# Graph attention with conditional features: the setup of a one-core kernel re-planned

## The chip, the cores and the metric

The kernel runs on one core of a Trainium2 chip. The metric is the device time of one execution in microseconds (us); the time of a kernel is the median of its runs. The engines of the core that matter here are TensorE (PE in the profile, with its weight loads as PEld), VectorE (DVE), ScalarE (ACT), GpSimd (POOL) and SyncE (SP), which in this kernel issues nearly all DMAs. Each engine takes its instructions in the order in which the program lists them for it.

## The reference

There are 16 batches of 512 nodes with 512 features, 16 heads of width 32, and two relations d. Only the first 20 nodes of a batch act as keys and values. Cut to what matters:

```python
row_zero = v.sum(-1) == 0                       # a node whose features sum to zero
q_exp = where(row_zero[..., None], 0.0, q[:, None, :])
self_feat = concat([v, q_exp], -1) @ W_self.T + b_self
output = self_feat
for d in range(2):
    A = (adj if d == 0 else swapaxes(adj, 1, 2))[:, :, :20, :]
    mask, bias = A.sum(-1) > 0, A @ w_bias + b_bias
    kv = self_feat[:, :20]
    qh = self_feat @ Wq[d].T + bq[d]            # split over heads
    kh = kv @ Wk[d].T + bk[d]                   # split over heads
    w = softmax(where(mask, qh . kh / sqrt(32), NEG) + bias)
    output += per_head(w @ kv) @ Wout[d] + bout[d]
return v + relu(output)
```

The condition vector q enters each node's features by one term, W_self's second half times q, which is dropped for nodes whose row sum is zero. The kernel holds that decision as a *row flag* per node (0 or 1). All arithmetic is in float32.

## The kernel before

**What is done once.** The query projection is folded into the keys: for every batch, the 20 keys of both relations and all 16 heads are multiplied by Wq once, so that the scores of a node are one product of its self features with a table g of 512 x 640 per batch. The setup (lines 347 to 630) makes these tables for all 16 batches, the value rows, a bias term per key, and half of the self features of batch 0. The main loop (from line 658) then runs over 16 batches b and four tiles nt of 128 nodes: it makes the self features of the tiles to come (`self_feat`), the scores of this tile, softmax, and in tile 2 the attention output of the batch before.

**The order is by hand.** The program stands in `tc.manual_schedule()`: every engine executes in the order of the text. A tile buffer is one of `bufs` slots of its tag, handed out in turn; an instruction that writes to a slot waits until all that used the slot's former tile is done, DMAs included.

**The setup's stages.**

- *Front.* SP loads the key nodes' features `xkv` and the weights `ws_v` in four pieces of 128 rows, with the condition `q_sb`, its weights `ws_q` (1 MB) between pieces 1 and 2 (lines 394 to 414), and then everything else: key weights, query weights, x of batch 0, adjacency, output weights, x of batch 1 (`load_x(1)`, line 415). Eight matmuls on constants keep TensorE busy meanwhile (line 384). The key nodes' features accumulate in `kv_ps`; between pieces 1 and 2 stands the product of q with `ws_q` (line 435).
- *Key rows.* `key_rows(d, jc)` (line 470): four matmuls of 128x320 into a bank of `ps_acc`, which ScalarE moves to `khT`. There are eight.
- *Bursts.* `keys(runs)` (line 543): the 64 halves of the table are taken three at a time, so there are 22 bursts, 0 to 21, the last with one half. A burst fills two PSUM pairs (`ps_s`, both of its buffers). ScalarE then empties pair 0 and VectorE pair 1 into a stage tile `st` (lines 563 to 569), and the next burst can begin only when both are empty. When a stage is full, SP writes its share of batch 0 to `g0` in SBUF, of batch 1 to `g1_d` and of the other 14 batches to `g_d`, both in DRAM (lines 572 to 576). `st` has four slots.
- *Gaps.* What lies on TensorE between bursts n and n+1 I call gap n. Until burst 4 it is filled by key rows, each just ahead of the burst that needs it (line 604). From gap 4 on, a list `other` (lines 583 to 587) is spread evenly by a count (line 612): `biases`, row flags, `bias_scores` for both relations, `self_step` (half of a bank of self features), `values`, and batch 1's row flags.

**Names that the steps below touch.**

- `bias_scores(d)` (line 501): four small matmuls, a ScalarE copy into a tile of tag `full` (two slots), and four DMAs on GpSimd's queue to `cq_d`.
- `values(t, ds, k)` (line 517): one matmul of 128x512 for each k; after the last k VectorE copies the bank to a tile of the same tag `full`, and GpSimd's queue writes it to `vw_d`. `bias_terms` and `full_add` use the tag `full` too.
- `row_sums(b)` (line 163) adds the four chunks of x on GpSimd; `row_flags(b)` (line 170) multiplies the result with ones on TensorE and compares on VectorE. Later batches do it another way: `load_xn`, `row_sum` on ScalarE, `row_mask`, and through DRAM back with `load_nz` (lines 90, 148, 154, 159).
- `mask_count`, `mask_mul`, `mask_add` (lines 207 to 232) prepare the adjacency of half a batch; `mask_add` ends with four copies on ScalarE, which wait for two VectorE instructions.
- After the setup SP goes on with `load_keys(1)` (line 639), which waits for the last write to `g1_d`, and with the loads of tiles 1 and 2 of batch 0.

Of the kernel before, what the change touches and what calls it, by code (L numbers as in the profile page):

```python
# [13 lines left out]
P = 128  # L14
# [4 lines left out]
def gat_kernel(  # L19
# [60 lines left out]
    nz_d = dram.tile([B, N], F32, name="nz_d")  # L80

    xs, xns, rss, adjs, nzs, sfs, cqs, gs, vds = {}, {}, {}, {}, {}, {}, {}, {}, {}
    adds, fulls, wts, outs, held, sf_ps, conds, prods = {}, {}, {}, [], [None], {}, {}, {}


    def load_x(b):
        xs[b] = load.tile([P, C, N], F32, tag="x", name=f"x{b}", bufs=4)
        nc.sync.dma_start(xs[b], xT[b].rearrange("(c p) n -> p c n", p=P))
# [74 lines left out]
    def row_sums(b):  # L163

        t = rss[b] = load.tile([P, 2, F], F32, tag="xn", name=f"rx{b}")[:, 0]
        nc.gpsimd.tensor_add(t, xs[b][:, 0], xs[b][:, 1])
        for k in range(2, C):
            nc.gpsimd.tensor_add(t, t, xs[b][:, k])
# [65 lines left out]
    def full_add(b, nt):  # L234
        f = fulls[b, nt] = msk.tile([P, H * S], F32, tag="full", name=f"full{b}_{nt}").rearrange(
            "p (g h m) -> p g h m", g=2, m=S
        )
        shape = [P, 2, H // 2, S]
        nc.gpsimd.tensor_add(  # L239
            f, cqs[b].unsqueeze(1).to_broadcast(shape),  # L240
            adds[b, nt // 2][:, nt % 2].unsqueeze(2).to_broadcast(shape),
        )
# [104 lines left out]
    with tc.tile_pool(name="setup", bufs=1) as sp:  # L347
# [18 lines left out]
        with tc.tile_pool(name="setup_k", bufs=1) as sk:  # L366
# [14 lines left out]
                    base=-k * DH, channel_multiplier=1,  # L381
                )
            warm = ps_acc.tile([P, 512], F32, tag="acc", name="ps_warm")
            for _ in range(8):
                nc.tensor.matmul(warm[:, :P], ones, ones, start=True, stop=True)

            def rows(sb, src):
                nc.sync.dma_start(sb, src.rearrange("(c p) f -> p c f", p=P))

            def kv_rows(k, n):  # L390
                rows(xkv[:, k : k + n], xkvT[k * P : (k + n) * P])
                rows(ws_v[:, k : k + n], wsT[k * P : (k + n) * P])

            kv_rows(0, 1)
            kv_rows(1, 1)
            nc.sync.dma_start(q_sb, qT)
            rows(ws_q, wsT[F:])
            kv_rows(2, 1)
            kv_rows(3, 1)
            nc.sync.dma_start(bs_sb, b_self)  # L400
            for d in range(2):
                rows(wk_sb[d], wkT[d])
            nc.sync.dma_start(bk_sb, bk)
            for d in range(2):
                rows(wq_sb[:, d], wq[d])
            nc.sync.dma_start(br_sb, b_row.partition_broadcast(P))
# [5 lines left out]
            nc.sync.dma_start(bo_sb, bout)  # L412
            for d in range(2):
                rows(wo_sb[:, d], woT[d])
            load_x(1)
            load_adj(0, 1)


# [80 lines left out]
        with tc.tile_pool(name="setup_g", bufs=4) as sg:  # L499
# [17 lines left out]
            def values(t, ds, k):  # L517


                rows = min(P, BM - t * P)  # L520
                if k == 0:
                    held[0] = ps_acc.tile([P, 512], F32, tag="acc", name=f"ps_v{t}{ds[0]}")
                ps = held[0]
                for i, d in enumerate(ds):
                    nc.tensor.matmul(  # L525
                        ps[bass.ds(i * rows, rows)], kvT[:, k, bass.ds(t * P, rows)], wo_sb[:, d, k],
                        start=(k == 0), stop=(k == C - 1),
                    )
                if k == C - 1:
                    v = msk.tile([P, H * S], F32, tag="full", name=f"v{t}{ds[0]}")[:, :F].rearrange(  # L530
                        "p (e c g) -> p e c g", c=C, g=DH
                    )
                    nc.vector.tensor_copy(v, ps.rearrange("p (c e g) -> p e c g", c=C, g=DH))
                    for i, d in enumerate(ds):
                        nc.gpsimd.dma_start(
                            vw_d[d, bass.ds(t * P, rows)],
                            v[bass.ds(i * rows, rows)].rearrange("p e c g -> p (e c g)"),
                        )
# [4 lines left out]
            def keys(runs):  # L543


                pairs = [ps_s.tile([P, 2, 512], F32, tag="s", name=f"ps_g{runs[0]}{i}") for i in range(2)]
                at = 0
                for fc, hg, d, lo, hi in runs:
                    n = (hi - lo) * HB * NG
                    for hl in range(HL):  # L550
                        r = bass.ts(hl, DH)
                        nc.tensor.matmul(  # L552
                            pairs[hl // 2][:, hl % 2, at : at + n], wq_sb[r, d, hg, bass.ts(fc, P)],
                            khT[r, d * C + hg, lo * HB * NG : hi * HB * NG], start=True, stop=True,
                        )
                    at += n
                at = 0
                for fc, hg, d, lo, hi in runs:
                    n = (hi - lo) * HB * NG
                    if (fc, hg) not in stages:  # L560
                        stages[fc, hg] = sg.tile([P, B, HL, 2, NG], F32, tag="st", name=f"st{fc}{hg}")
                    st = stages[fc, hg]
                    for half in range(2):
                        to = st[:, lo * HB : hi * HB, bass.ts(half, 2), d].rearrange("p b h m -> p h b m")
                        of = pairs[half][:, :, at : at + n].rearrange("p h (b m) -> p h b m", m=NG)
                        if half == 0:
                            nc.scalar.activation(to, of, AF.Copy, scale=SCALE)
                        else:
                            nc.vector.tensor_scalar(to, of, SCALE, None, ALU.mult)
                    at += n  # L570
                    if d == 1 and hi == 2:
                        nc.sync.dma_start(
                            g0[:, fc, bass.ts(hg, W // C)], st[:, 0].rearrange("p h d m -> p (h d m)")
                        )
                        nc.sync.dma_start(g1_d[C * fc + hg], st[:, 1].rearrange("p h d m -> p (h d m)"))
                        nc.sync.dma_start(g_d[C * fc + hg], st[:, 2:])

            def self_step(b, f, h, i, k):
                self_feat(b, f, h, ((i, (k, k + 1)),))
                if (i, k) == (1, C - 2):  # L580
                    self_copy(b, f, h)

            other = [(biases, ()), (row_flags, (0,)), (bias_scores, (0,)), (bias_scores, (1,))]
            other += [(self_step, (0, 0, 0, i, k)) for i in range(2) for k in (0, 2)]
            other += [(values, (t, (d,), k)) for t in range(2) for d in range(2) for k in range(C)]
            other += [(values, (2, (0, 1), k)) for k in range(C)] + [(row_flags, (1,))]
            other += [(self_step, (0, 1, 0, i, k)) for i in range(2) for k in (0, 2)]

            halves = [(fc, hg, d, i) for fc in range(C) for hg in range(C) for d in range(2) for i in range(2)]
            bursts = []  # L590
# [7 lines left out]
                bursts.append(runs)  # L598
            rest = [(d, hg) for hg in range(C) for d in range(2)]
            first = None  # L600
            done = 0
            for n, runs in enumerate(bursts):
                for i in range(len(rest)):
                    if i < (3 if n == 0 else 1) or any(fc == 0 and (d, hg) == rest[0] for fc, hg, d, _, _ in runs):
                        key_rows(*rest.pop(0))
                keys(runs)
                if rest:
                    for d in range(2):
                        bias_terms(d, n)
                    continue  # L610
                first = n if first is None else first
                while done * (len(bursts) - first) < (n + 1 - first) * len(other):
                    f, args = other[done]
                    f(*args)
                    done += 1
                if n == 6:
                    mask_count(0, 0)
                if n == 7:
                    mask_mul(0, 0)
                if n == 9:  # L620
                    mask_add(0, 0)
                    load_cq(0)
                if n == 11:
                    row_sums(1)
                if n == 13:
                    mask_count(0, 1)
                if n == 15:
                    mask_mul(0, 1)
                if n == 18:
                    full_add(0, 0)  # L630

    soft = ctx.enter_context(tc.tile_pool(name="soft", bufs=2))
    gp = ctx.enter_context(tc.tile_pool(name="gp", bufs=2))
# [3 lines left out]
    gs[0] = g0  # L637
    with tc.manual_schedule():
        load_keys(1)

        def side(t, lo, hi, q):

# [15 lines left out]
        for b in range(B):  # L658
# [13 lines left out]
            for nt in range(NT):  # L672
                store()
                if nt == 1:
                    if b + 1 < B:
                        load_adj(b + 1, 0)
                        load_cq(b + 1)
                    if b == 0:
                        clear_blocks(zero)
                        blocks()  # L680
                if nt == 2:
# [176 lines left out]
```

## Time and profile before

| | us |
|---|---|
| median of 3 runs | 633.07 (631.02, 633.38, 633.07) |
| profiled execution, its time | 631.96 |
| its span, first to last instruction | 630.0 |
| end of burst 21 on TensorE | 90.84 |
| one batch of the main loop on TensorE (starts of tile 2's scores at 140.57 and 173.91) | 33.34 |

The profiled execution lies 1.1 us under the median of the runs, and 1.96 us of it lie outside its span. Times inside the profile are counted from the start of the span. A row of an engine's timeline gives the start, the time from there to the end of the last of the merged instructions, engine, line, operation, the tile written and those read, shape, and how many instructions; float32 matmuls appear as two instructions each. What stands in brackets is the idle time before and what ended it. TensorE matmuls overlap and their ends are modelled, so the time that a piece of work takes is better read from its start to the start of the next piece than from its duration.

### The profile page before, as it was taken

How to read it: one execution, taken by the hardware profiler on the slowest of the kernel's cores; microseconds unless marked ns; L12 is line 12 of the kernel's file. 1: busy time of each engine (PE TensorE's matmuls, PEld its weight loads, DVE VectorE, ACT ScalarE, POOL GpSimd, SP SyncE). 2: the span in 40 equal slices, each digit the busy share in tenths (PEclk: the TensorE clock that was granted, in tenths of full speed). 3: DMA queues.
4: the chain of work that ended last, by engine and by line, in shares of the span. 5: the costliest groups of instructions: out<-in, count | busy, mean ns of one | idle time of the engine just before them, and what ended most of it. 6: DMA issues, size and time to landing. Idle time of an engine off the chain costs nothing.

```text
span 630.0 us, 16419 instructions
## 1 busy us (share of the span) xinstructions
PE 622.3 (99%) x6834; PEld 371.0 (59%) x6834; DVE 505.6 (80%) x809; ACT 218.2 (35%) x480; POOL 340.7 (54%) x263
## 2 busy tenths in 40 slices
PE   8999999999999999999999999999999999999997
PEld 6655455656565656565565656565656565655554
DVE  0566556888888888889888979798888888888896
ACT  1444421233242424242423334333424242424341
POOL 2405331546646473839293847465564747382973
PEclk9999999999999999999999999999999999999999
DMA  8999998627375475729291918294756557482513
GB/s 278 395 378 328 388 371 265 211 100 256 147 215 189 128 277 118 286 58 347 40 362 21 347 43 300 100 257 147 232 171 186 218 138 266 89 316 50 182 52 118
DMA packets 89553, 131.86 MB, mean 209 GB/s; under 512 B 8872, under 2 KB 59592, under 8 KB 87432
## 3 DMA queue, kind: packets, MB, share of 16 engines
q1 hardware_dynamic: 88808, 129.47, 61.4%
q0 software_dynamic: 672, 1.36, 0.8%
q8 instruction: 53, 0.87, 0.6%
q14 instruction: 20, 0.16, 0.1%
HBM read 90.89 MB, written 39.92 MB: 208 GB/s over the span
## 4 chain that ended last, share of the span: by engine, by line
PE 87%; DVE 0%; issue 0%; DVEq 0%
PE ps_s L254 44%; PE ps_sf L189 33%; PE ps_o L316 7%; PE ps_v L525 1%; PE ps_o L651 1%; PE ps_s L247 0%; PE ps_nz L172 0%; PE ps_g(3, 1, 1, 0, 2)0_724 L552 0%; PE ps_g(3, 3, 0, 0, 2)0_778 L552 0%; PE ps_g(3, 2, 0, 1, 2)0_752 L552 0%; PE ps_g(3, 0, 1, 1, 2)0_701 L552 0%; PE ps_g(3, 0, 0, 0, 2)1_682 L552 0%; PE ps_g(3, 0, 0, 0, 2)0_681 L552 0%; DVE o L790 0%; PE ps_g(3, 3, 1, 1, 2)0_801 L552 0%
## 5 line engine op out<-in xcount | busy, mean ns | idle before, releaser
L254 PE MATMUL ps_s<-g,sf 128*64 128x320 f32 x2048 | 287.4, 433 | 0.0
L189 PE MATMUL ps_sf<-x,ws_v 128*64 128x256 f32 (+1 forms) x2048 | 221.4, 371 | 0.0
L254 PEld LDWEIGHTS ps_s<-g,sf 128*64 128x64 f32 x2048 | 145.6, 137 | 125.7 <-issue 7.1
L189 PEld LDWEIGHTS ps_sf<-x,ws_v 128*64 128x64 f32 x2048 | 146.6, 137 | 71.9 <-issue 1.7
L298 POOL TENSOR_TENSOR s<-s,sm 128x640 f32<-128x640 f32 x63 | 80.2, 1273 | 140.5 <-DVE sm L297 129.6
L274 ACT ACTIVATE s<-s 128x640 f32<-128x640 f32 x63 | 46.5, 737 | 218.1 <-DVE s L269 218.1
L239 POOL TENSOR_TENSOR full<-cq,both 128x640 f32<-128x640 f32 x64 | 99.1, 1549 | 27.1 <-ACT both L230 22.1
L211 POOL TENSOR_TENSOR prod<-prod,wb_sb 128x880 f32<-128x880 f32 x32 | 61.4, 1918 | 56.4 <-ACT prod L210 56.4
L265 DVE TENSOR_TENSOR ps_s<-ps_s,full 128x640 f32<-128x640 f32 x63 | 52.3, 831 | 38.9 <-PE ps_s L254 37.4
L338 POOL TENSOR_TENSOR o<-o,x 128x512 f32<-128x512 f32 x60 | 75.5, 1279 | 1.1 <-ACT o L335 1.1
L230 ACT COPY both<-add 64x80 f32<-64x80 f32 x128 | 32.8, 256 | 77.4 <-DVE add L225 76.3
L202 DVE SCALAR_TENSOR_TENSOR sf<-nz,qw,ps_sf 128x236 f32<-128x236 f32 (+1 forms) x128 | 52.6, 459 | 3.5 <-PE ps_sf L189 3.5
L335 ACT ACTIVATE o<-o,bo 128x512 f32<-128x512 f32 x60 | 40.0, 714 | 44.3 <-DVE o L329 44.3
L296 DVE TENSOR_REDUCE sm<-s 128x32 f32<-128x640 f32 x63 | 51.6, 818 | 4.4 <-ACT s L274 0.9
L267 DVE TENSOR_REDUCE mx<-ps_s 128x32 f32<-128x640 f32 x63 | 51.9, 825 | 2.2
L269 DVE TENSOR_TENSOR s<-ps_s,mx 128x640 f32<-128x640 f32 x63 | 51.9, 824 | 2.2
L305 DVE STREAM_TRANSPOSE wt<-s 128x640 f32<-128x640 f32 x63 | 52.5, 834 | 0.6 <-POOL s L298 0.6
L316 PE MATMUL ps_o<-wt,vd 32*32 32x256 f32 (+2 forms) x2176 | 45.3, 372 | 0.6 <-issue 0.6
L316 PEld LDWEIGHTS ps_o<-wt,vd 32*32 32x32 f32 x2176 | 30.0, 103 | 16.1 <-issue 8.2
L329 DVE TENSOR_TENSOR o<-ps_o,sf 128x512 f32<-128x512 f32 x60 | 36.3, 667 | 0.0
L152 ACT ACTIVATE xn<-xn 128x512 f32<-128x512 f32 x56 | 34.3, 613 | 0.0
L216 DVE TENSOR_REDUCE cond<-adj 128x80 f32<-128x880 int32 x32 | 33.1, 1034 | 0.0
(210 smaller groups left out, 424.6 us busy)
## 6 DMA issues: line engine op xcount, KB each, us to landing
g<-g_d SPq DMA_DIRECT2D x15, 1280.0 KB, 8.7
g_d<-st SPq DMA_DIRECT2D x16, 1120.0 KB, 6.2
x<-in_xT SPq DMA_DIRECT2D x16, 1024.0 KB, 11.0
out_T<-o SPq DMA_DIRECT2D x60, 256.0 KB, 4.6
xn<-in_xn SPq DMA_DIRECT2D x28, 512.0 KB, 8.4
adj<-in_adj SPq DMA_DIRECT2D x32, 440.0 KB, 7.3
vd<-bd_d SPq DMA_DIRECT2D x64, 128.0 KB, 4.0
nz<-nz_d SPq DMA_DIRECT2D x14, 256.0 KB, 4.5
```

Source lines behind the costliest of these rows:

```text
L189: nc.tensor.matmul(held[0][bass.ts(a, R), i * N // 2 : i * N // 2 + hi - lo], ws_v[:, k, bass.ds((2 * f + i) * P + a * R, R)], xs[b][:, k, ...
L202: nc.vector.scalar_tensor_tensor(sfs[b][:, 2 * f + i, lo:hi], nzs[b][:, lo:hi], qw[:, 2 * f + i, b : b + 1], ps[:, i * N // 2 : i * N // 2 ...
L211: nc.gpsimd.tensor_mul(p, p, wb_sb.unsqueeze(1).to_broadcast([P, 2 * S, L]))
L239: nc.gpsimd.tensor_add(f, cqs[b].unsqueeze(1).to_broadcast(shape), adds[b, nt // 2][:, nt % 2].unsqueeze(2).to_broadcast(shape),)
L254: nc.tensor.matmul(bank[bass.ts(a, R), : W // 2], sfs[b][:, k, bass.ds(nt * P + g * R, R)], keys[:, k, a], start=start and k == 0, stop=(k ...
L265: nc.vector.tensor_add(pw, pw, fulls.pop((b, nt)).rearrange("p g h m -> p g (h m)"))
L267: nc.vector.tensor_reduce(mx, p4, AX.X, ALU.max)
L269: nc.vector.tensor_sub(s, p4, mx.unsqueeze(3).to_broadcast(full))
L298: nc.gpsimd.tensor_mul(s, s, sm.unsqueeze(3).to_broadcast(full))
L305: nc.vector.transpose(wts[b][:, nt], s.rearrange("p a h m -> p (a h m)"))
L316: nc.tensor.matmul(banks[q][bass.ts(e, DH)].rearrange("p (t n) -> p t n", n=32), vds[b][r, e, i, q // 2 * 2 + n], wt[r, :, bass.ts(j, 32)] ...
L338: nc.gpsimd.tensor_add(o[:, c], o[:, c], xs[b][:, c])
```

## The change

It touches the setup and two places in batch 0 of the main loop.

- The warm-up has seven matmuls in place of eight. The first two pieces of `ws_v` and the two small biases `bs_sb` and `bk_sb` are loaded from ScalarE's queue, and the two biases come earlier.
- Four key rows stand ahead of burst 0 in place of three, so each is made one burst before it is needed.
- The list of other work gives way to six kinds of steps and a plan with one word for each gap from gap 4 on: b biases, c bias scores, n row flags of batch 0, s a quarter of a bank of self features (each of i, k), v values of tiles 0 and 1, w values of tile 2. Accumulators of self features, values of tiles 0 and 1, and values of tile 2 are held apart (`held`), so that they may interleave.
- The copy of batch 0's keys into `g0` is made by GpSimd in place of a DMA.
- Batch 1's row flags come as in later batches: `load_xn` after bursts 10 and 12, `row_sum` on ScalarE after bursts 15 to 18, `row_mask` after burst 19, and `load_nz(1)` in tile 1 of batch 0. `row_sums(1)` and the matmul for them go.
- `load_x(1)` moves from the front's queue to just after `load_keys(1)`.
- The steps of the masks move: `mask_count(0, 0)` from burst 6 to 7, `mask_mul` from 7 to 8, `mask_add` and `load_cq` from 9 to 10, the second `mask_count` from 13 to 12 and `mask_mul` from 15 to 14.

```diff
@@ -80,7 +80,7 @@
     nz_d = dram.tile([B, N], F32, name="nz_d")
 
     xs, xns, rss, adjs, nzs, sfs, cqs, gs, vds = {}, {}, {}, {}, {}, {}, {}, {}, {}
-    adds, fulls, wts, outs, held, sf_ps, conds, prods = {}, {}, {}, [], [None], {}, {}, {}
+    adds, fulls, wts, outs, held, sf_ps, conds, prods = {}, {}, {}, [], [None] * 3, {}, {}, {}
 
 
     def load_x(b):
@@ -381,26 +381,27 @@
                     base=-k * DH, channel_multiplier=1,
                 )
             warm = ps_acc.tile([P, 512], F32, tag="acc", name="ps_warm")
-            for _ in range(8):
+            for _ in range(7):
                 nc.tensor.matmul(warm[:, :P], ones, ones, start=True, stop=True)
 
-            def rows(sb, src):
-                nc.sync.dma_start(sb, src.rearrange("(c p) f -> p c f", p=P))
-
-            def kv_rows(k, n):
-                rows(xkv[:, k : k + n], xkvT[k * P : (k + n) * P])
-                rows(ws_v[:, k : k + n], wsT[k * P : (k + n) * P])
-
-            kv_rows(0, 1)
-            kv_rows(1, 1)
+            def rows(sb, src, queue=nc.sync):
+                queue.dma_start(sb, src.rearrange("(c p) f -> p c f", p=P))
+
+            def kv_rows(k, queue=nc.sync):
+                rows(xkv[:, k : k + 1], xkvT[bass.ts(k, P)])
+                rows(ws_v[:, k : k + 1], wsT[bass.ts(k, P)], queue)
+
+
+            kv_rows(0, nc.scalar)
+            kv_rows(1, nc.scalar)
+            nc.scalar.dma_start(bs_sb, b_self)
+            nc.scalar.dma_start(bk_sb, bk)
             nc.sync.dma_start(q_sb, qT)
             rows(ws_q, wsT[F:])
-            kv_rows(2, 1)
-            kv_rows(3, 1)
-            nc.sync.dma_start(bs_sb, b_self)
+            kv_rows(2)
+            kv_rows(3)
             for d in range(2):
                 rows(wk_sb[d], wkT[d])
-            nc.sync.dma_start(bk_sb, bk)
             for d in range(2):
                 rows(wq_sb[:, d], wq[d])
             nc.sync.dma_start(br_sb, b_row.partition_broadcast(P))
@@ -412,7 +413,6 @@
             nc.sync.dma_start(bo_sb, bout)
             for d in range(2):
                 rows(wo_sb[:, d], woT[d])
-            load_x(1)
             load_adj(0, 1)
 
 
@@ -519,8 +519,8 @@
 
                 rows = min(P, BM - t * P)
                 if k == 0:
-                    held[0] = ps_acc.tile([P, 512], F32, tag="acc", name=f"ps_v{t}{ds[0]}")
-                ps = held[0]
+                    held[1 + t // 2] = ps_acc.tile([P, 512], F32, tag="acc", name=f"ps_v{t}{ds[0]}")
+                ps = held[1 + t // 2]
                 for i, d in enumerate(ds):
                     nc.tensor.matmul(
                         ps[bass.ds(i * rows, rows)], kvT[:, k, bass.ds(t * P, rows)], wo_sb[:, d, k],
@@ -569,22 +569,27 @@
                             nc.vector.tensor_scalar(to, of, SCALE, None, ALU.mult)
                     at += n
                     if d == 1 and hi == 2:
-                        nc.sync.dma_start(
+                        nc.gpsimd.tensor_copy(
                             g0[:, fc, bass.ts(hg, W // C)], st[:, 0].rearrange("p h d m -> p (h d m)")
                         )
                         nc.sync.dma_start(g1_d[C * fc + hg], st[:, 1].rearrange("p h d m -> p (h d m)"))
                         nc.sync.dma_start(g_d[C * fc + hg], st[:, 2:])
 
             def self_step(b, f, h, i, k):
-                self_feat(b, f, h, ((i, (k, k + 1)),))
-                if (i, k) == (1, C - 2):
+                self_feat(b, f, h, ((i, (k,)),))
+                if (i, k) == (1, C - 1):
                     self_copy(b, f, h)
 
-            other = [(biases, ()), (row_flags, (0,)), (bias_scores, (0,)), (bias_scores, (1,))]
-            other += [(self_step, (0, 0, 0, i, k)) for i in range(2) for k in (0, 2)]
-            other += [(values, (t, (d,), k)) for t in range(2) for d in range(2) for k in range(C)]
-            other += [(values, (2, (0, 1), k)) for k in range(C)] + [(row_flags, (1,))]
-            other += [(self_step, (0, 1, 0, i, k)) for i in range(2) for k in (0, 2)]
+
+            steps = {
+                "b": [(biases, ())],
+                "c": [(bias_scores, (d,)) for d in range(2)],
+                "n": [(row_flags, (b,)) for b in range(1)],
+                "s": [(self_step, (0, f, 0, i, k)) for f in range(2) for i in range(2) for k in range(C)],
+                "v": [(values, (t, (d,), k)) for t in range(2) for d in range(2) for k in range(C)],
+                "w": [(values, (2, (0, 1), k)) for k in range(C)],
+            }
+            plan = "bvv vv cc vv vv n sss sss vv ssw vv vv vv www sss sss ss".split()
 
             halves = [(fc, hg, d, i) for fc in range(C) for hg in range(C) for d in range(2) for i in range(2)]
             bursts = []
@@ -598,10 +603,9 @@
                 bursts.append(runs)
             rest = [(d, hg) for hg in range(C) for d in range(2)]
             first = None
-            done = 0
             for n, runs in enumerate(bursts):
                 for i in range(len(rest)):
-                    if i < (3 if n == 0 else 1) or any(fc == 0 and (d, hg) == rest[0] for fc, hg, d, _, _ in runs):
+                    if i < (4 if n == 0 else 1) or any(fc == 0 and (d, hg) == rest[0] for fc, hg, d, _, _ in runs):
                         key_rows(*rest.pop(0))
                 keys(runs)
                 if rest:
@@ -609,25 +613,28 @@
                         bias_terms(d, n)
                     continue
                 first = n if first is None else first
-                while done * (len(bursts) - first) < (n + 1 - first) * len(other):
-                    f, args = other[done]
+                for kind in plan[n - first] if n - first < len(plan) else ():
+                    f, args = steps[kind].pop(0)
                     f(*args)
-                    done += 1
-                if n == 6:
+                if n == 7:
                     mask_count(0, 0)
-                if n == 7:
+                if n == 8:
                     mask_mul(0, 0)
-                if n == 9:
+                if n == 10:
                     mask_add(0, 0)
                     load_cq(0)
-                if n == 11:
-                    row_sums(1)
-                if n == 13:
+                if n in (10, 12):
+                    load_xn(1, n // 2 - 5)
+                if 15 <= n < 19:
+                    row_sum(1, n - 15)
+                if n == 12:
                     mask_count(0, 1)
-                if n == 15:
+                if n == 14:
                     mask_mul(0, 1)
                 if n == 18:
                     full_add(0, 0)
+                if n == 19:
+                    row_mask(1)
 
     soft = ctx.enter_context(tc.tile_pool(name="soft", bufs=2))
     gp = ctx.enter_context(tc.tile_pool(name="gp", bufs=2))
@@ -637,6 +644,7 @@
     gs[0] = g0
     with tc.manual_schedule():
         load_keys(1)
+        load_x(1)
 
         def side(t, lo, hi, q):
 
@@ -676,6 +684,7 @@
                         load_adj(b + 1, 0)
                         load_cq(b + 1)
                     if b == 0:
+                        load_nz(1)
                         clear_blocks(zero)
                         blocks()
                 if nt == 2:
```

## What I expect of it, before seeing its time

> **What bounds the kernel.** I read the page's busy shares and slices first, then TensorE's timeline through the setup, then who ends its waits.
>
> ```profile
> PE 622.3 (99%) x6834; PEld 371.0 (59%) x6834; DVE 505.6 (80%) x809; ACT 218.2 (35%) x480; POOL 340.7 (54%) x263
> ...
> PE   8999999999999999999999999999999999999997
> ```
>
> TensorE is busy in every slice but the first and the last, so time can be won only by taking work from it or by closing holes. The change leaves the main loop's work as it is (33.34 us of TensorE for a batch), so I price the setup: from the start to the end of burst 21 (90.84) and the one self step behind it (0.9), 91.7 us.
>
> "Busy" hides holes there, because ends of matmuls are modelled. I take starts. A burst takes 1.02 us (53.63 less 52.61) when nothing holds it; a gap with two value matmul pairs 1.91 (55.54 less 53.63).
>
> ```profile
> 11.42 1.05 PE L435 MATMUL ps_q<-ws_q,q_sb 128*16 128x512 f32 x8 [1.43 <-DMA ws_q<-in_wsT]
> ```
>
> ```profile
> 42.62 1.13 PE L172 MATMUL ps_nz<-rx,ones 128*128 128x512 f32 x2
> ...
> 45.16 1.28 PE L505 MATMUL ps_c<-khT,bqbd 128*32 128x320 f32 x16
> ...
> 61.47 0.41 PE L552 MATMUL ps_g(2, 0, 0, 1, 2)0_569<-khT,wq_sb 32*128 32x160 f32 x2 [0.38 <-ACT st L567]
> ...
> 85.59 1.13 PE L172 MATMUL ps_nz<-rx,ones 128*128 128x512 f32 x2
> ```
>
> The reader is to see the front's wait for `ws_q`, the two row-flag matmuls, and a burst that waits for ScalarE's emptying. Emptying takes ScalarE 1.03 us and VectorE 1.22, begins about 0.1 to 0.2 after the burst, and so asks for a gap of about 1.5 us; a shorter one shows as a longer burst (gap 4 is 1.19, burst 5 then 1.35).
>
> **1. Rows one burst ahead: −0.7.** Bursts 2, 3 and 4 took 1.17, 1.44 and 1.17, as their keys' `khT` came late (TensorE waits for ScalarE's L478 inside them). One burst ahead, `khT` is there: 0.15 + 0.42 + 0.15.
>
> **2. Batch 1's row flags off TensorE: −1.0.** From 85.59 to the next start, 86.64. In its place ScalarE gets four row sums (0.61 plus 0.19 for the read in the main loop, 0.7 apart), one a burst. It needs 1.03 of some 2.9 us of a burst and gap, so they fit. Their loads are issued five bursts (some 15 us) ahead; x and xn rows land 8 to 11 us after issue. The three GpSimd adds (4 us) that go were off the path.
>
> **3. Old losses in gaps that go: −2.8.** Gap 4 and burst 5: 0.15 + 0.33; burst 6: 0.70; single values in gaps 9 and 15 (1.19 for 1.0 of work) with bursts 10 and 16: 2 x 0.53; gap 10 and burst 11 behind `mask_add`: 0.45 + 0.10.
>
> **4. New short gaps: +1.6.** A quarter self step is 0.42, a word adds 0.06. Against 1.5: cc (1.22) 0.27, n (1.04) 0.32, sss (1.32) 0.17 three times (the fourth is in step 5), ss (0.90) 0.6: 1.7, less 0.1 as VectorE is not always late. All vv, ssw and www gaps are long enough.
>
> **5. mask_add before a short gap: +1.1.** These rows are VectorE's and ScalarE's around gap 9 and 10 of before:
>
> ```profile
> 57.87 1.06 DVE L223 TENSOR_REDUCE lb<-prod 128x80 f32<-128x880 f32 x1
> 58.96 0.30 DVE L225 SCALAR_TENSOR_TENSOR add<-cond,bb_sb,lb 128x80 f32<-128x80 f32 x1
> ```
>
> ```profile
> 59.30 1.06 ACT L230 COPY both<-add 64x80 f32<-64x80 f32 x4 [1.59 <-DVE add L225]
> 60.38 1.03 ACT L567 ACTIVATE st<-ps_g(1, 3, 1, 0, 2)0_545 128x640 f32<-128x640 f32 x2
> ```
>
> The copies end 1.3 us after the burst (59.11) that ScalarE should be emptying, and a 1.91 gap still lost 0.45. After the change the same stands between bursts 10 and 11, and gap 11 is sss, 1.32: 1.32 − 1.91 makes it 0.6 worse. About 1.1, with its share of burst 12.
>
> **6. A new wait: c1 for the first values' write: +1.9.** Before, tag `full` went bias terms, c0, c1, v. Now it goes bias terms, v(0,0) in gap 5, c0, c1 in gap 6. With two slots c1 takes v(0,0)'s, and its copy, on ScalarE, must wait until that tile's write to `vw_d` has landed. Behind it stand the emptying of burst 7, and burst 8 waits for that.
>
> ```profile
> vw_d<-v POOLq DMA_DIRECT2D x4, 256.0 KB, 4.7
> ```
>
> From T, the end of gap 5: VectorE copies from 0.1 to 0.8, GpSimd issues at 1.1 (0.3 after a copy's end, as 61.33 follows 61.04), landing 4.7 later at 5.8, c1's copy (0.43) to 6.25, emptying (1.03) to 7.3. Burst 8 would have started at T + 1.02 + 1.49 + 1.02 + 1.91 = 5.45. Loss 1.9. The six writes of before landed 3.15 to 5.64 after issue: 0.3 to 2.8. I take the median.
>
> **7. Front: −0.9 (bounds −1.6 and +0.3).** SP issues a load each 0.47 us and `ws_q` sixth, at 3.08; with two `ws_v` pieces on ScalarE's queue it is fourth, at about 2.1. By the trace's landing times `ws_q` was there at 11.29 and `ws_v`'s third piece at 12.41, and TensorE went on at 11.42 and 12.55; all to 18.36 follows. Windows of 1 us, with DMA share and GB/s last:
>
> ```profile
> 4.00:5.00 1.00, 1.00 (x5) 0.97 (x5) 0.00 (x0) 0.00 (x0) 0.00 (x0) 1.00 0.78 219
> 5.00:6.00 1.00, 1.00 (x3) 0.64 (x2) 0.00 (x0) 0.00 (x0) 0.50 (x1) 1.00 0.48 125
> ```
>
> The row: between 4 and 8 us the DMA engines idled some 1.2 us in all, just where `ws_q` should have begun, so an earlier issue is worth its 0.95. [...] I take the row, since the engines were idle there. The bounds: all of the idle time and 0.4 for the shorter warm-up, −1.6; or no gain, and `ws_q` held up by the two small biases (384 packets, some 9 ns each in the trace) and by sharing with the second queue, +0.3. The shorter warm-up itself I put at nothing: the first piece starts 0.43 sooner, but the first of its matmuls run at half pace whatever the clock row says (0.53 apart until 6.2, 0.27 after), and its end (9.8) is hidden by the wait for `ws_q`. If that wait shrank below it, 0.2 to 0.4 would show.
>
> **8. At nothing.** The 16 copies to `g0`: no such row; GpSimd's nearest, 128x320 with two inputs, takes 0.72 to 0.87, so I put 128x160 with one at 0.4, 6 us in all on an engine with 340 of 630 busy; the last is read at 95.1. Cover gone, the scores of tile 0 wait for some tenths. It takes 1.3 MB from queues that are 0.9 to 1.0 busy from 40 to 90 us. SP loses 16 issues of 0.5 and waits that go with them. `load_x(1)`: SP reaches `load_keys(1)` at 96.98 and the keys landed at 103.3; x1 (1 MB, 2.7 us at 390 GB/s) lands near 106, and TensorE reads it at 111.5. Behind it the adjacency (104.7 before), cq, blocks and x2 move by 3 us; the nearest user, ScalarE's cast of batch 1's adjacency, met its second half just as it landed (126.75) and its next work was at 132.8. `load_nz(1)` is read at 119.4. The stages' four slots: a write lands 6.2 after issue and a slot is asked for again after 15.
>
> **Sum:** −0.7 −1.0 −2.8 +1.6 +1.1 (of step 5) +1.9 −0.9 = −0.8. The profiled execution would go from 631.96 to 631.2, the median of the runs, 1.1 above it, from 633.07 to **632.3**.
>
> **Rivals.**
>
> *A. The gain without the new wait* (0.2). Less stands in the queues around 47 us (no x1), so the write lands in 3.2 and c1 costs 0.3; the front gives 1.6. Sum −0.8 −1.6 −0.7 = −3.1: 630.0. For it: the idle time of the front; against it: six landings with only one under 3.8.
>
> *B. The software queue decides* (0.2). v(0,0)'s write lands 5.6 or later, so c1 costs 2.8 or more, and the front gives nothing: −0.8 +0.9 +0.9 = +1.0, to 634.1. With the front at nothing it is slower than before as soon as the write takes over 4.6 us. For it: the two last writes took 3.8 and 5.6 while DMA was full[...].
>
> *C. x1 comes late* (0.1). Until 111.5 it costs nothing; then each us is one of TensorE. `x` landed 11.0 after issue by the page's median, at 108.4 from here; only a keys' load that waits for stage writes much later would bring it to 116 and the time to 637.
>
> *D. Another small effect of either sign* (0.1).
>
> **Chances.** Forecast 0.4. Half a per cent is 3.2 us, about what a measurement can tell from no change: faster would be under 629.9, slower over 636.2. Faster takes half of A and some of D: 0.16. Slower takes C and a tail of B: 0.14. The rest, 0.70, is no change. The range, 629.7 to 635.0, holds the forecast's bounds (−3.1 to +1.0) and a little of the spread of runs (2.4).
>
> **What would show it.** Bursts 2 to 4 at 1.02 us; no L172 matmul after the first; `ws_q` ending the front's wait at about 10.5, not 11.4; a burst 8 held by ScalarE, whose copy L510 waited for `vw_d`; a burst 12 held by L230; tile 3 of batch 0 on TensorE without a wait for x. I am wrong if burst 8 starts 1.9 after burst 7, or if TensorE shows idle time after 100 us.

## The result, and the profile after

The changed kernel takes 636.66 us (median of 9 runs, 634.68 to 639.11) against 633.05 (9 runs, 630.95 to 635.18): a ratio of 1.0073 with an interval of 1.0055 to 1.009, so it is slower by 0.7%. The forecast was 632.3, within 629.7 to 635.0. The profiled execution took 638.12, with a span of 635.3. These two lines of the page give the busy shares and TensorE's slices, and the third the granted clock in the same slices:

```profile
PE 623.3 (98%) x6830; PEld 371.6 (58%) x6830; DVE 506.7 (80%) x809; ACT 220.6 (35%) x488; POOL 342.3 (54%) x276
...
PE   8998999979999999999999999999999999999997
...
PEclk9999999989999999999999999999999999999999
```

Two slices of TensorE have fallen: the fourth (48 to 64 us) by a tenth, and the ninth (127 to 143 us) by two, with the clock. The setup, which I had priced, is not where the time went: it ends earlier than before. Cut on TensorE's timeline at three starts and at the end of its last matmul, the two profiled executions compare so:

| us | before | after | difference |
|---|---|---|---|
| start of `ws_q`'s product (front) | 11.42 | 10.47 | −0.95 |
| from there to the first scores of batch 0 (rest of the setup) | 83.72 | 83.25 | −0.47 |
| from there to the scores of tile 2 of batch 1 | 45.36 | 51.43 | **+6.07** |
| from there to TensorE's last matmul | 485.71 | 486.00 | +0.29 |
| from there to the end of the span | 3.79 | 4.15 | +0.36 |
| outside the span | 1.96 | 2.82 | +0.86 |
| sum | 631.96 | 638.12 | +6.16 |

The third row holds the loss. TensorE's timeline of after, in that stretch:

```profile
131.98 4.48 PE L254 MATMUL ps_s<-g,sf 128*64 128x320 f32 x32
137.15 0.70 PE L316 MATMUL ps_o<-wt,vd 32*32 32x256 f32 x6 [0.69 <-DVE wt L305]
140.75 4.47 PE L316 MATMUL ps_o<-wt,vd 32*32 32x256 f32 x122 [2.90 <-issue]
145.15 4.91 PE L254 MATMUL ps_s<-g,sf 128*64 128x320 f32 x32
```

L316 is the attention output of batch 0. Before, its 128 matmuls stood in one piece of 2.75 us:

```profile
137.82 2.75 PE L316 MATMUL ps_o<-wt,vd 32*32 32x256 f32 x128
```

Now six run, TensorE stands still for 2.90 us, and the rest takes 4.47. "Issue" says that the profile names no releaser, so VectorE's timeline is read beside it:

```profile
125.33 0.35 DVE L297 RECIPROCAL sm<-sm 128x32 f32<-128x32 f32 x1
130.07 1.07 DVE L216 TENSOR_REDUCE cond<-adj 128x80 f32<-128x880 int32 x1 [4.39 <-DMA adj<-in_adj]
131.18 1.93 DVE L217 TENSOR_SCALAR cond<-cond 128x80 f32<-128x80 f32 x1
133.02 0.86 DVE L202 SCALAR_TENSOR_TENSOR sf<-nz,qw,ps_sf 128x256 f32<-128x256 f32 x2
...
136.26 0.83 DVE L305 STREAM_TRANSPOSE wt<-s 128x640 f32<-128x640 f32 x1
...
139.78 0.86 DVE L202 SCALAR_TENSOR_TENSOR sf<-nz,qw,ps_sf 128x256 f32<-128x256 f32 x2
```

VectorE's mask count (L216) waited 4.39 us for the second half of batch 1's adjacency. Behind it in the text stand the self copies (L202), the softmax, and the transposition of tile 3's weights (L305), which the attention output reads: that is the 0.69. It then needs four banks of `ps_acc`, which has four, and the second pair of self copies empties the last of them; it goes on 0.1 after that pair's end (139.78 + 0.86). The three other kernels with such a hole, further down, show the same 0.1. Before, L216 did not wait: the first row below is its row of before. The second and third are SyncE's issue of that half, before and after:

```profile
127.02 1.01 DVE L216 TENSOR_REDUCE cond<-adj 128x80 f32<-128x880 int32 x1
120.44 0.50 SPq L96 DMA_DIRECT2D adj<-in_adj  x1
122.46 0.50 SPq L96 DMA_DIRECT2D adj<-in_adj  x1
```

Before, the half landed 6.3 us after its issue, at 126.75: a margin of 0.27 us. Now it was issued 2.0 later and took 7.6, to 130.05, while TensorE was ahead by 1.4.

Two windows of this execution, with the granted clock as the third value from the end, show why the rest took 4.47 instead of 2.7:

```profile
138.00:141.00 3.00, 0.25 (x16) 0.28 (x32) 2.96 (x6) 1.35 (x6) 1.27 (x1) 0.69 0.01 3
141.00:146.00 5.00, 5.00 (x126) 2.96 (x101) 3.60 (x6) 1.97 (x6) 1.54 (x1) 0.50 0.01 3
```

The clock was at half (0.50) while the rest ran. So the 6.07 are 0.75 up to the start of the attention output, 2.90 of standing still, and 2.42 of slower work, most of it at half clock.

### The profile page after: what moved, and what is told of

Its sections match the earlier page's. It is cut to its first block, busy times and chain, and to the rows that moved or that the text cites. A ratio compares the mean times of both kernels' runs of the same rounds, so it can differ in the third digit from the quotient of the medians.

```text
span 635.3 us, 16421 instructions
## 1 busy us (share of the span) xinstructions
PE 623.3 (98%) x6830; PEld 371.6 (58%) x6830; DVE 506.7 (80%) x809; ACT 220.6 (35%) x488; POOL 342.3 (54%) x276
## 4 chain that ended last, share of the span: by engine, by line
PE 80%; DMA 5%; SPq 2%; issue 1%; DVE 1%; ACT 0%; POOL 0%; DVEq 0%; POOLq 0%
PE ps_s L254 40%; PE ps_sf L189 29%; PE ps_o L316 7%; DMA adj<-in_adj 3%; PE ps_v L525 1%; SPq L145 1%; DMA vw_d<-v 1%; DMA g_d<-st 1%; PE ps_o L659 1%; SPq L88 0%; DMA bd_d<-vw_d 0%; SPq L117 0%; PE ps_s L247 0%; DVE st L569 0%; DVE cond L216 0%
## 5 line engine op out<-in xcount | busy, mean ns | idle before, releaser
L298 POOL TENSOR_TENSOR s<-s,sm 128x640 f32<-128x640 f32 x63 | 80.1, 1271 | 143.7 <-DVE sm L297 129.7
L202 DVE SCALAR_TENSOR_TENSOR sf<-nz,qw,ps_sf 128x236 f32<-128x236 f32 (+1 forms) x128 | 52.6, 458 | 3.1 <-PE ps_sf L189 3.1
L305 DVE STREAM_TRANSPOSE wt<-s 128x640 f32<-128x640 f32 x63 | 52.5, 834 | 0.9 <-POOL s L298 0.9
L316 PE MATMUL ps_o<-wt,vd 32*32 32x256 f32 (+2 forms) x2176 | 47.7, 386 | 4.1 <-issue 3.4
L316 PEld LDWEIGHTS ps_o<-wt,vd 32*32 32x32 f32 x2176 | 31.1, 105 | 20.6 <-issue 11.4
L152 ACT ACTIVATE xn<-xn 128x512 f32<-128x512 f32 x60 | 36.9, 614 | 0.0
L216 DVE TENSOR_REDUCE cond<-adj 128x80 f32<-128x880 int32 x32 | 33.2, 1037 | 4.4 <-DMA adj<-in_adj 4.4
```

The costliest lines, as they stand in the source:

```text
L202: nc.vector.scalar_tensor_tensor(sfs[b][:, 2 * f + i, lo:hi], nzs[b][:, lo:hi], qw[:, 2 * f + i, b : b + 1], ps[:, i * N // 2 : i * N // 2 ...
L298: nc.gpsimd.tensor_mul(s, s, sm.unsqueeze(3).to_broadcast(full))
L305: nc.vector.transpose(wts[b][:, nt], s.rearrange("p a h m -> p (a h m)"))
L316: nc.tensor.matmul(banks[q][bass.ts(e, DH)].rearrange("p (t n) -> p t n", n=32), vds[b][r, e, i, q // 2 * 2 + n], wt[r, :, bass.ts(j, 32)] ...
```

## The experiments

Three theories stood at the start. **L**, late adjacency: the hole above. **V**, late value rows: the chain of clears and copies that makes `vd`, which also came later (issued at 120.22, before 117.86). **Q**: the second DMA queue costs time by itself.

**Is it the adjacency?** The first four runs, timed beside 54 runs of the kernel before (632.01).

*x of batch 1 back in the front.*

```diff
+            load_x(1)
             load_adj(0, 1)
...
         load_keys(1)
-        load_x(1)
```

> The changed kernel with x of batch 1 back in the front's queue (one line back). Theory L (late adjacency: x1 behind the keys pushes batch 1's second adjacency half, on which VectorE waits 4.4 us ahead of the softmax, so that TensorE finds no free bank for the attention of batch 0): VectorE's wait for adj at line 216 falls under 1.5 us, TensorE has no hole near 137 us, the span goes from 635.3 to about 629, 1 under before's 630.0. Rival V (the value rows vd arrive late through the longer chain of clear and block DMAs): the hole goes too, as that chain also starts 3 us sooner. Rival Q (a second DMA queue in the program costs about 1 us around the span, and the rest is lost in the setup): span no better than 633; time less span stays about 2.9 under Q and also under L, as the queue is still there.

Measured: 633.95 (22 runs), ratio 1.003 [1.0013, 1.0046]. Some 2.7 us of the loss went, not all of it. VectorE's wait and TensorE's hole became shorter but stayed:

```profile
129.57 1.07 DVE L216 TENSOR_REDUCE cond<-adj 128x80 f32<-128x880 int32 x1 [2.97 <-DMA adj<-in_adj]
```

```profile
140.24 3.58 PE L316 MATMUL ps_o<-wt,vd 32*32 32x256 f32 x122 [2.31 <-issue]
```

So the place of x alone is not what makes the half late. With x in front it still landed at 129.54, 2.8 later than in the kernel before: SyncE issued it at 121.73, 1.3 later, and it took 7.8 us, 1.5 longer. The keys' load, which waits for the setup's last writes, was issued at 97.18, against 95.44 in the changed kernel: x ahead of the setup's writes costs part of what x behind them does. One load in this chain is new in the changed kernel and in this one, `load_nz(1)` (0.53 us of SyncE, 256 KB). No run takes it out, so its share of the 2.8 is not known, and what makes up the rest stays open.

*That half alone brought forward*, into tile 1 of batch 0.

```diff
                         load_cq(b + 1)
                     if b == 0:
+                        load_adj(1, 1)
                         load_nz(1)
...
-                    if b + 1 < B:
+                    if 0 < b < B - 1:
                         load_adj(b + 1, 1)
```

> The changed kernel, x1 late as it is, but batch 1's second adjacency half is loaded right behind its first half. Theory L: the half lands near 109 in place of 130, VectorE does not wait, no hole at 137: span about 629 to 630. Rival V: the value chain is one load longer than in the changed kernel, so the hole stays or grows by 1 us: span 635 to 637. Rival Q: no change, 635.

Measured: 632.37 (14 runs), ratio 1.0002 [0.999, 1.0015]. VectorE's timeline, and TensorE's below it:

```profile
126.84 1.01 DVE L216 TENSOR_REDUCE cond<-adj 128x80 f32<-128x880 int32 x1
127.89 0.52 DVE L217 TENSOR_SCALAR cond<-cond 128x80 f32<-128x80 f32 x1
```

```profile
137.63 2.75 PE L316 MATMUL ps_o<-wt,vd 32*32 32x256 f32 x128
```

No wait, no hole, and the stretch from the first scores to tile 2 of batch 1 is 45.36 again, as before. The value rows were issued later still (122.23): **V falls**. Whatever made the half late, its lateness is the loss.

*The two mask steps of that half moved behind the softmax*, so that nothing of VectorE's stands behind the wait.

```diff
-                if nt == 0 and b > 0:
+                if nt == 0 and b > 1:
                     mask_mul(b, 1)
                     mask_count(b, 1)
...
                         turn(*prev)
+                    if nt == 0 and b == 1:
+                        mask_mul(b, 1)
+                        mask_count(b, 1)
```

> The changed kernel with all loads as they are; only in tile 0 of batch 1 the two mask steps that read the second adjacency half (line 210 on ScalarE, 216 on VectorE) stand behind the softmax's first part and the transpose. Theory L: VectorE does the self copies, softmax and transpose first, the adjacency still lands near 130 but is asked for later; the hole at 137 shrinks from 3.6 us to under 1 and the slow clock after it goes: span about 630. Rival V: the hole stays, 635. Rival Q: 635.

Measured: 634.52 (17 runs), ratio 1.0035 [1.0022, 1.0048]. L216 (131.94) waits for no transfer now, but it and L217 stand 3 us ahead of the self copy whose bank TensorE needs, and a hole of 1.70 is left, not one under 1 as expected, with the clock at 1.00 behind it:

```profile
136.29 0.63 PE L316 MATMUL ps_o<-wt,vd 32*32 32x256 f32 x6
138.62 2.69 PE L316 MATMUL ps_o<-wt,vd 32*32 32x256 f32 x122 [1.70 <-issue]
```

*The two queues and the seven warm-ups alone, on the kernel before.*

```diff
-            for _ in range(8):
+            for _ in range(7):
...
-            kv_rows(0, 1)
-            kv_rows(1, 1)
+            kv_rows(0, nc.scalar)
+            kv_rows(1, nc.scalar)
+            nc.scalar.dma_start(bs_sb, b_self)
+            nc.scalar.dma_start(bk_sb, bk)
```

> The kernel before with the front's part of the change alone: two pieces of ws_v and the two small biases on ScalarE's queue, seven warm-ups. By the changed kernel's profile TensorE goes on at 10.47 in place of 11.42, so the span should fall by about 1.0 to 629.0. Theory L says nothing of time around the span. Rival Q: time less span grows from 1.96 to about 2.9, so the gain is given back and the time is that of before within 0.3. If Q is false the time falls by 1.0.

Measured: 632.40 (14 runs), ratio 0.9998 [0.9981, 1.0016]. **Q is not the loss**, and the front brings no gain in the time either.

*Both places at once*: the half in tile 1, and x of batch 1 in the front (the two edits above together; the comparison has 58 runs of before, 632.03).

> The changed kernel with both edits: x of batch 1 back in the front's queue, and batch 1's second adjacency half loaded in tile 1. Theory 'late adjacency': only the arrival of that half mattered, so the position of x1 costs nothing either way: 632.4 within 0.6, no wait of VectorE at its first mask count of that half, and the attention output of batch 0 in one piece of about 2.75 us. Rival 'x1 crowds the setup's writes': the last key write to DRAM lands later, the loads behind it too, and the median is 633.5 or more.

Measured: 632.30 (22 runs), ratio 0.9993 [0.998, 1.0006]. With the half early, the place of x does not matter.

*The reverse: the kernel before, with only that half made late.*

```diff
-                    if b + 1 < B:
+                    if 0 < b < B - 1:
                         load_adj(b + 1, 1)
                     if b + 2 < B:
                         load_xn(b + 2, 0)
                         load_xn(b + 2, 1)
+                    if b == 0:
+                        load_adj(1, 1)
```

> The kernel before, with one edit: in tile 2 of batch 0 the load of batch 1's second adjacency half stands behind both loads of xn of batch 2 (1 MB more in front of it), nothing else. Theory 'late adjacency': it lands 2.5 to 3.5 us later than 126.75, VectorE waits for it at its first mask count, TensorE meets a hole of 2 to 3 us in the attention output of batch 0, and the time rises by 3 to 5 us: 635 to 637. Rival 'late value rows or the setup's own plan': this half is not what counts, and the time stays at 632.0 within 0.7.

Measured: 634.85 (12 runs) against 632.76 (30 runs) beside it, ratio 1.0035 [1.0017, 1.0053]. VectorE's wait, then TensorE's hole, of the very same length as in the changed kernel:

```profile
130.53 1.07 DVE L216 TENSOR_REDUCE cond<-adj 128x80 f32<-128x880 int32 x1 [3.76 <-DMA adj<-in_adj]
131.64 1.92 DVE L217 TENSOR_SCALAR cond<-cond 128x80 f32<-128x80 f32 x1
```

```profile
137.60 0.70 PE L316 MATMUL ps_o<-wt,vd 32*32 32x256 f32 x6
141.21 2.69 PE L316 MATMUL ps_o<-wt,vd 32*32 32x256 f32 x122 [2.90 <-issue]
```

**L is shown from both sides**: late in the kernel before, the half makes the hole; early in the changed one, it takes it away. The time rose by 2.1, under the 3 to 5 expected. The hole was as long as expected, but here the rest of the attention output ran at full clock, 2.69. Of the two profiled executions this one's stretch to tile 2 of batch 1 is 4.09 longer and its span 3.2, mostly as its front was 0.73 shorter; the medians of the spans differ by 2.0.

**What the other steps are worth.** All four runs rest on the kernel with the half early (632.37).

*No wait of the copy c1*: the bias scores go to slots of the tag `nz`.

```diff
-                t = msk.tile([P, H * S], F32, tag="full", name=f"c{d}")[:, :BM]
+                t = load.tile([P, N], F32, tag="nz", name=f"c{d}")[:, :BM]
```

> The changed kernel with batch 1's second adjacency half loaded early (as in the run that loads it in tile 1, 632.37), and besides the two bias-score copies c0 and c1 put into slots of the tag nz, so that ScalarE's copy c1 no longer waits for the write of v(0,0) to land. Theory 'the wait is on the path': gap 7 falls from 3.44 to about 1.9 us, the end of the setup comes 1.5 us earlier, the median about 630.9 and the span about 627.9. Rival 'the transfers of batch 0 decide': gap 7 falls just as much, but a wait in batch 0 takes it back, and the median stays at 632.0 to 632.6.

Measured: 630.89 (19 runs), ratio to the kernel before 0.9965 [0.9954, 0.9976]. ScalarE's timeline without the edit (first fence) and with it:

```profile
48.59 0.43 ACT L510 COPY c<-ps_c 128x320 f32<-128x320 f32 x1
52.13 0.43 ACT L510 COPY c<-ps_c 128x320 f32<-128x320 f32 x1 [3.11 <-DMA vw_d<-v]
52.46 1.04 ACT L567 ACTIVATE st<-ps_g(1, 1, 0, 1, 2)0_453 128x320 f32<-128x320 f32 x2
```

```profile
48.57 0.77 ACT L510 COPY c<-ps_c 128x320 f32<-128x320 f32 x2
49.95 1.03 ACT L567 ACTIVATE st<-ps_g(1, 1, 0, 1, 2)0_453 128x320 f32<-128x320 f32 x2 [0.61 <-PE ps_g(1, 1, 0, 1, 2)0_453 L552]
```

The two copies run together, the emptying of burst 7 begins 2.5 sooner, and gap 7 falls from 3.44 to 1.91. The 1.5 us stay: nothing later took them back.

*Batch 0's keys by DMA instead of GpSimd.*

```diff
-                        nc.gpsimd.tensor_copy(
+                        nc.sync.dma_start(
                             g0[:, fc, bass.ts(hg, W // C)], st[:, 0].rearrange("p h d m -> p (h d m)")
```

> The changed kernel with the second adjacency half loaded early, and batch 0's keys written to g0 by SyncE's DMA as before instead of by GpSimd. If GpSimd's copies are what lengthens the time around the span (2.9 us where before has 2.0), time minus span falls to about 2.1 and the median to 631.5. If not, time minus span stays at 2.9. Inside the span the copies were taken at nothing: the span stays within 0.5 us of 629.4; if the copies were a gain or a loss, it moves by more.

Measured: 636.66 (6 runs), ratio 1.006 [1.0036, 1.0083]: 4.3 above the kernel with the copies on GpSimd, where nothing or a small gain was expected. The last share of `g0`, issued at 92.70, landed at 98.69, in the middle of the first scores, which read it (TensorE's timeline; 4.48 in one piece in the kernel before):

```profile
94.23 2.32 PE L254 MATMUL ps_s<-g,sf 128*64 128x320 f32 x14
98.82 2.61 PE L254 MATMUL ps_s<-g,sf 128*64 128x320 f32 x17 [2.27 <-DMA g<-st]
```

The stretch from the first scores on is 48.35 in place of 45.36, 3.0 of the 4.3. So GpSimd's copies are no idle edit: in this plan they keep the keys out of a queue in which they would arrive too late. Time minus span was 2.64, not the 2.1 expected if they alone lengthened it.

*The front of the kernel before* (one queue, eight warm-ups; the reverse of the diff of the two queues).

> The changed kernel with the second adjacency half loaded early, and the front as before: both pieces of ws_v and the two biases on SyncE's queue, eight warm-up matmuls. The forecast's row [...] says +0.9: 633.3, with ws_q's product starting about 1 us later than with two queues. [...]

Measured: 631.87 (22 runs), ratio to before 0.9994 [0.998, 1.0007]: no loss. The median span is 0.5 longer than with two queues (629.85 against 629.35), and time minus span 0.9 shorter (2.07 against 2.94).

*All that helps together*: half early, `c` in `nz`, and the old front.

> The changed kernel with three edits: the second adjacency half loaded early, the bias-score copies in slots of the tag nz, and the front of the kernel before (one queue, eight warm-up matmuls). If the three are independent: 630.89 with the first two, less 0.5 (631.87 against 632.37 for the front alone) = 630.4, with time minus span at 2.1 instead of 3.1. Rival 'the front's second queue does start the setup earlier by 0.6 to 1.0 us, and that counts once nothing behind it waits': 631.0 or more.

Measured: 630.85 (19 runs), ratio 0.9971 [0.9957, 0.9986] to the kernel before. The 0.5 us from the old front did not add up: with `c` in `nz`, one queue (630.85) and two (630.89) are alike. Either is faster than both kernels, by 0.3% than before and by some 0.9% (630.89 / 636.66) than the changed one.

The starts on TensorE's timeline of all profiled executions, one each:

| | `ws_q`'s product | to the first scores | to tile 2 of batch 1 | median us |
|---|---|---|---|---|
| before | 11.42 | 83.72 | 45.36 | 632.0 to 633.1 |
| changed | 10.47 | 83.25 | 51.43 | 636.66 |
| x in front | 10.66 | 83.97 | 49.12 | 633.95 |
| half early | 10.89 | 84.07 | 45.36 | 632.37 |
| masks behind | 9.60 | 84.01 | 47.63 | 634.52 |
| two queues alone | 10.18 | 83.61 | 45.35 | 632.40 |
| half early, x in front | 10.94 | 84.00 | 45.36 | 632.30 |
| half early, c in `nz` | 11.08 | 82.25 | 45.36 | 630.89 |
| half early, g0 by DMA | 10.42 | 83.81 | 48.35 | 636.66 |
| half early, one queue | 11.14 | 82.98 | 45.36 | 631.87 |
| all three | 10.40 | 82.25 | 45.36 | 630.85 |
| before, half late | 10.69 | 83.69 | 49.45 | 634.85 |

The middle columns repeat to some hundredths wherever nothing waits, while the front scatters by over 1 us.

## Why the prediction was wrong

**The step that failed is 8, "At nothing"**, in what it says of the moved `load_x(1)`. It named the right transfer and its landing (126.75) and took "the nearest user, ScalarE's cast of batch 1's adjacency" with "its next work at 132.8" as the cover. ScalarE had cover. VectorE's mask count reads the same half, stood at 127.02, 0.27 after the landing, and has the self copies, tile 3's softmax and, through them, a PSUM bank of TensorE behind it. I counted one reader of a transfer that has two, and the second is on the engine that is 80% busy. The step let the setup end sooner and the transfer come later without setting the two against each other: the reader came 1.4 us earlier (VectorE was free at 125.68 in place of 127.10) and the data 3.3 later, 4.7 in all against a margin of 0.27, which is the wait of 4.39. Its price was 6.1 in the profiled execution, not nothing, and some 4.3 in the medians (636.66 against 632.37). TensorE's idle time after 100 us, which the prediction named as a sign of being wrong, is this hole.

The delay itself ("move by 3 us") had the right size, 3.3, but in part by luck. It was put down to the moved x, and with x back in the front the half was still 2.8 late. `load_nz(1)` stood in the same step with only its own reader priced, not what it does to the loads behind it; its share is not measured.

**Rival C gave 637, and that is no merit**: its mechanism, TensorE waiting for x itself, did not happen. x landed at 105.97 and was read at 110.09 without a wait.

The other steps, by the columns above:

- **Steps 1 to 6, +0.1 in all.** Where c1's wait was full (five profiles, 83.81 to 84.07) the stretch to the first scores was 0.1 to 0.35 longer than before, and without the wait 1.47 shorter; my sum without it was −1.8. In the changed kernel's own profile, where c1 waited less, it was 0.47 shorter. There, bursts 2 and 3 took 1.02 and 1.03, as said, but burst 4 1.17 and not 1.02. Gap 11 took 2.35 in place of 1.32, and burst 12 1.12: the 1.1 of step 5.
- **Step 6, c1: +1.9, bounds 0.3 and 2.8.** The mechanism was as told. The size was 1.0 in the changed kernel's profile (gap 7 of 2.82 in place of 1.91, burst 8 0.10 longer) and 1.6 to 1.7 in five others with two queues. It follows the landing of v(0,0)'s write: 3.8 us after issue in the first, 4.4 in the kernel with the half early (1.6), where I had put 4.7. Taking the wait away brought 1.48 us of time.
- **Step 7, the front: −0.9 by the row, 0 in the time.** The changed kernel's profile shows −0.95, just as the row had it, and that is the trap. The kernel before starts that product at 11.42 in one execution; the same front started it at 10.69, 10.40 and 11.14 in the three others. Four fronts with one queue have a mean of 10.91, eight with two 10.53: 0.4 for the second queue, inside a scatter of 1.0 to 1.5. And in the time it is 0: 632.40 against 632.01, 632.37 against 631.87, 630.89 against 630.85.
- **Step 8, g0: at nothing.** True for the change as made; that a DMA in its place would have cost 4.3 I did not see.
- **Outside the span** I took the execution's 1.96 as given. It became 2.90 (median of 9), and this 0.9 is why even the kernel with the half early only equals the one before, with a span 0.55 shorter.

So for the setup and its front, −0.8 stands against −1.4 in the profiled execution. The result was decided behind them, by one margin of 0.27 us in the main loop.

## What to carry to other kernels

When a load moves, list *every* instruction that reads what lies behind it in its queue, on every engine, with its start and the landing before it; the smallest difference is the margin, and a setup that gets faster uses up the same margin from the other end. Price a blown margin by what stands behind the waiting instruction on its engine, to the PSUM bank that TensorE needs. And take no front that waits for one DMA from a single execution: repeat it, or give it the scatter.

## What the runs showed of the hardware

**With a hole of 2.90 us TensorE's clock fell to half in one execution, and not in another.** The changed kernel and the kernel with the late half have the same hole (2.90). In these windows of the latter, one execution too, the clock stays at 1.00, where the changed kernel's had 0.69 and 0.50:

```profile
138.00:141.00 3.00, 0.30 (x6) 0.00 (x0) 2.93 (x6) 1.36 (x7) 1.27 (x1) 1.00 0.00 0
141.00:146.00 5.00, 4.79 (x138) 3.02 (x140) 3.59 (x7) 2.42 (x7) 1.55 (x1) 1.00 0.01 3
```

Narrow windows place the fall. In the changed kernel the clock is at half from 139.1 to 146.0, 6.8 us: it is 1.00 from 139.0 to 139.1, 0.50 from 140.0 to 140.75 and 1.00 again from 146.0 on, so it fell inside the hole, which lasted to 140.75. With x in front, after a hole of 2.31 that ended at 140.24, the mean clock from 138 to 146 was 0.79, and 1.00 from 110 to 138 and from 146 to 174. With the masks behind, where the hole was 1.70, it was 1.00 in all three stretches. Each of these is one execution.

Six of the changed kernel's nine runs had a mean clock under 0.998, with a median span of 635.1 against 632.8 for the other three. Such a mean alone is no mark of the hole: 44 of the 142 runs of the kernel before that were timed with the experiments have it too, but only 3 of 69 runs of the four kernels with two queues in which TensorE met no hole (two queues alone, and the half early with or without x in front or `c` in `nz`).

**VectorE's L217 lasts until an instruction of GpSimd ends.** In the profiles of before and of the changed kernel it takes 0.20 where GpSimd computes nothing beside it, and 0.51 or 0.52 at nearly every second of its places in the main loop. Behind the late half it took 1.92 to 1.96, and what it ends with is not in its brackets but on GpSimd's timeline:

```profile
131.13 1.92 POOL L211 TENSOR_TENSOR prod<-prod,wb_sb 128x880 f32<-128x880 f32 x1 [4.02 <-ACT prod L210]
```

This product ends at 133.05 and L217 (131.18 + 1.93) 0.06 later; in the kernel before with the half late it is 133.51 and 0.05. Where L217 took 0.51 or 0.52, it ended 0.05 to 0.07 after GpSimd's L298, at each of these places in the two profiles. The late half releases the cast and the mask count together, so product and L217 start 0.05 apart. Of the 4.5 us by which the self copy came late (133.02 against 128.50), 1.4 are this (1.93 in place of 0.52). The traces show that the two end together and what it costs, not what links them.

**Time around the span is not a constant.** Its median is 2.0 to 2.2 us for the kernel before and its two versions, two queues among them; 2.9 to 3.1 for the changed kernel and four of its versions, 2.6 for two more, and 2.1 to 2.3 for those with one queue. The second queue alone doesn't make it (2.12), and without GpSimd's copies it is still 2.64; what does, together with that queue, stays open.
